# A two-layer attention and mixture-of-experts block: products that nobody reads, another order of stored queries and keys, and another pace of six experts

## The chip, the core and the metric

One core of a Trainium2 chip runs the whole program. The time is device microseconds of that core; a single run is one execution. Five engines work side by side: TensorE (PE: the matmuls; PEld: the loads of their stationary operands), VectorE (DVE), ScalarE (ACT), GpSimd (POOL) and SyncE (SP, which here only issues transfers). The profile gives the clock granted to TensorE as a share of full speed, PEclk.

## The reference, cut to what matters

Batch 2, 2048 tokens, width 256, in float32. Layer 0 is causal attention with 16 query heads of 16 numbers, 4 key heads and rotary embedding, beside 8 experts of which each token takes two. Layer 1 is attention over 32 learned patterns with sparsemax, beside 8 small experts and a shared one.

```python
xn = layernorm(x)
q = rope((xn @ Wqa @ Wqb).reshape(b, s, 16, 16))
k, v = split((xn @ Wkva @ Wkvb).reshape(b, s, 4, 16, 2)); k = rope(k)
w = softmax(where(causal, q @ repeat(k, 4).T / 4, -inf))
attn0 = (w @ repeat(v, 4)) @ Wout + bout
ffn0  = sum over the token's 2 experts e: gate * ((gelu(xn @ Wa[e]) * (xn @ Wg[e])) @ W_out[e])
x = x + attn0 + ffn0
xn = layernorm(x)
x = x + sparsemax_attention(xn, 32 patterns) + routed_and_shared_mlp(xn)
```

## The kernel before, in words

The span has three stages. The first, up to about 1434 us, makes layer 0's attention, routes the tokens, and runs the first six of layer 0's eight experts (`NIN = 6`) between the attention's matmuls. The second, from about 1461 us, runs experts 6 and 7. The third is layer 1.

**The list of the first stage.** Every instruction of the first stage is pinned in program order. A Python loop at the end of the stage (L1458) writes that order with a small model of the engines: `T` holds the time up to which each engine is taken, `on` and `pe` move it on, and `later`/`flush` hold jobs of the other engines until they are ready. At each step `candidates` (L1357) offers the next piece of each kind with a cost, and the cheapest is written. The kinds are: `score` (L564, the tile `sc`, one matmul, then exp on ACT into `es`), `values` (L579, tile `av`, 4 heads side by side), `maxima` (L515, tile `s`, two heads side by side with 64 rows each, then a maximum on DVE), the preparation of each 512 tokens (`normed` with tile `tp`, `lows` with `lw`, `tables` with `cs`, `rope_products` with `pab`, `make_v` with `pv`, `project` with `po`), and the experts' pieces (`ext`, `exh`, `exy`). A switch of kind costs 200 ns in the model. The constants at L1080 weigh the kinds.

**Products that nobody reads.** `product` (L1430) writes one bf16 matmul of 256 columns on a tile of ones into a PSUM tile (`idle`) that nobody reads. `fill` (L1440) writes them only ahead of the experts' first piece, and only where the model sees TensorE without work: after the preparation's first tile one for each `EACH` = 160 ns of such time, where the model's busy time of TensorE in the last `COUNT` = 3413 ns is under `SHARE` = 0.6 of it. In this count every piece is busy for its whole time, switches included.

**Queries and keys.** A rotary product is split into a high and a low part (fp32r); scores are the sum of the four products of parts, so a head takes 64 rows. `write_q` (L501) and `write_k` (L486) store each part twice in DRAM (`qd`, `kd`), SP issuing the transfers; `load_q` (L504) and `load_k` (L489) read them back into the tiles `q` and `ks` in two transfers each. `clean_q` and `clean_k` (L353, L356) fill unused rows first; `sel16` (L347) and `onecol` (L350), two small constants for this, are made on DVE.

**The end of the first stage.** The last `values` are followed by two transposes on DVE, `project`, and `add_sum` (L617), which adds attention's rows to `x1` in DRAM by a transfer of the POOL queue (`x<-xo`). Experts' results are added to the same `x1` by `ex_send` (L795, `x<-low,tox`); these transfers follow one another. The pace of the experts is the term `ahead` at L1391: the share of their pieces written less the share of the scores written since they began.

Of the kernel before, what the change touches and what calls it, by code (L numbers as in the profile page):

```python
# [149 lines left out]
def moe_transformer_kernel(  # L150
# [142 lines left out]
    with ExitStack() as actx:  # L293
# [34 lines left out]
        qsl = [attw.tile([P, 4, 512], F32R, name=f"q{i}") for i in range(NQS)]  # L328
        qd = [dram.tile([P, 4, 512], F32, name=f"qd{i}") for i in range(16)]
        kd = [dram.tile([64, 4, 512], F32, name=f"kd{i}") for i in range(8)]  # L330

# [14 lines left out]

        V.tensor_copy(sel16, bc(ident[0:16, 0:16], 1, [16, 8, 16]))  # L347
        for g in range(4):
            r0 = 64 - 64 * (g % 2) + 2 * (g // 2)
            V.tensor_tensor(onecol[:, g:g + 1], ident[:, r0:r0 + 1], ident[:, r0 + 1:r0 + 2], ALU.add)  # L350


        def clean_q(i):  # L353
            pin(G.memset(qsl[i].bitcast(F32), 0.0))

        def clean_k(i):  # L356

            for g in range(4):
                pin(A.activation(ksl[i][:, g].rearrange("p (a n) -> p a n", n=P), bc(ones, 1, [P, 4, P]), AF.Copy,
                                 scale=onecol[:, g:g + 1]))  # L360
# [9 lines left out]
        pin(A.dma_start(wa_sb[:, :, 96:96 + NE], wg.rearrange("(c p) m -> p c m", p=P)))  # L370
        pin(SP.dma_start(wkv16[64:96, 0:8], wkvb[:, 0:256].rearrange("k (v c) -> k v c", c=32)[..., 0:16]))
        pin(SP.dma_start(wq16, wqb.rearrange("k v t (g c) -> k v (t g) c", g=4)[..., 0:16]))
        pin(SP.dma_start(wkv16[64:96, 8:12], wkvb[:, 256:320].rearrange("k (g c) -> k g c", c=16)))
# [6 lines left out]
        for h in range(2):  # L380
            for r in range(2):
                hp = slice(64 * h, 64 * h + 64)
                pin(G.tensor_copy(identh[hp, r, 64 * r:64 * r + 64], ident[hp, hp]))
        pin(G.tensor_copy(trih, trif))
        number = attw.tile([P, 2, NTILE], I32, name="number")
# [100 lines left out]
        def write_k(b, blk, part, r):  # L486
            sdma(kd[4 * b + blk][:, r::2], bc(part.bitcast(F32), 1, [64, 2, 512]))

        def load_k(b, blk, ks):  # L489
            kss[b, blk] = ks  # L490
            for a in range(2):
                rows = kd[4 * b + blk].rearrange("(b a d) r n -> a (d r) b n", a=2, d=16)
                sdma(ks[64 * a:64 * a + 64, a::2].bitcast(F32), rows[a])

# [6 lines left out]
        def write_q(jp, part, r):  # L501
            sdma(qd[jp][:, 2 * r:2 * r + 2], bc(part.bitcast(F32), 1, [P, 2, 512]))

        def load_q(j, q):  # L504
            qs[j] = q
            for a in range(2):
                rows = qd[j // 2].rearrange("(t b a d) r n -> t a (d r) b n", t=2, a=2, d=16)
                sdma(q[64 * a:64 * a + 64, a::2].bitcast(F32), rows[j % 2, a])

# [5 lines left out]
        def maxima(j, i, kb):  # L515

            qb = j // 4 % 4
            if (i, kb) == (0, 0):
                parts[j] = atp.tile([P, 4, 4, 4], F32, tag="part", bufs=3, name="part")
            ks, q = kss[j // 16, kb], qs[j]  # L520
            n = 512 if kb < qb else P * (i + 1)
            tiles = []
            for pair in range(2):
                sc = ps2.tile([P, 2, 512], F32, tag="ps2", name="s1")
                tiles.append(sc)
                for h in range(2):
                    g = 2 * pair + h
                    mm(sc[:, h, :n], lhsT=q[half(g), g, P * i:P * i + P], rhs=ks[half(g), g, :n],
                       start=True, stop=kb < qb)
# [26 lines left out]
        def place_max(j):  # L556

            for a in range(2):
                r0 = 64 - 64 * a
                sdma(qs[j][r0:r0 + 4, a::2].bitcast(F32), bc(mrs[j][4 * a:4 * a + 4].bitcast(F32), 1, [4, 2, 512]))  # L560

        ess, avs, t3s, t3cs, rcs, atts, xos = {}, {}, {}, {}, {}, {}, {}

        def score(j, c, g):  # L564

            b, qb = j // 16, j // 4 % 4
            lo = max(0, c - 4 * qb) * P
            n = 512 - lo
            if g % 2 == 0:
                ess[j, c, g // 2] = esp.tile([P, 2, 512], F32, tag="es", name="es")  # L570
            es = ess[j, c, g // 2]
            sc = pssc.tile([P, 512], F32, tag="sc", name="sc")
            mm(sc[:, :n], lhsT=kss[b, c // 4][:, g, c % 4 * P:c % 4 * P + P], rhs=qs[j][:, g, lo:512], start=True, stop=True)
            pin(A.activation(es[:, g % 2, :n], sc[:, :n], AF.Exp, scale=0.25))  # L574
            if c >= 4 * qb and g % 2 == 1:
                pin(G.affine_select(es[:, :, 0:P], es[:, :, 0:P], pattern=[[0, 2], [1, P]], compare_op=ALU.is_ge,  # L576
                                    fill=0.0, base=0, channel_multiplier=-1))
# [227 lines left out]
        INF = 10 ** 9  # L805
        HOP, SWITCH, ISSUE, LAND, BYTE = 150, 200, 620, 2300, 0.003
        FULL = dict.fromkeys(("t", "l", "p", "f", "o"), "sc")
        T = dict.fromkeys(("PE", "V", "A", "G", "S", "D"), 0)
# [5 lines left out]
        def on(eng, dur, ready=0):  # L814
            T[eng] = max(T[eng], ready) + dur
            if eng == "PE":
                streamed.append((T[eng] - dur, T[eng]))
            return T[eng] + HOP

        def pe(mode, dur, ready=0):  # L820
            mode = FULL.get(mode, mode)
            dur += SWITCH * (mode != model["mode"])
            model["mode"] = mode
            return on("PE", dur, ready)

# [11 lines left out]
        def flush():  # L837
            now, done = T["PE"], False
            for job in sorted(jobs, key=lambda z: z[:2]):
                rank, _, eng, dur, ready, f, then = job  # L840
                if ready > now or (eng == "S" and T["S"] > now + ISSUE):
                    continue
                if eng == "AV":
                    eng = "A" if T["A"] <= T["V"] else "V"
# [70 lines left out]
        def start_fetch(grp):  # L915
# [3 lines left out]
            def landed(t):  # L919
# [5 lines left out]
                def go(k, t):  # L925
                    if k == len(steps):
                        at["x", grp] = t
                        later("S", ISSUE, t, lambda: keep_rows(grp), lambda t: x_done(grp, t), 2)
                    else:
                        if k < 6:  # L930
                            later("G" if k == 5 and grp > 1 else "V", costs[k], t, steps[k],
                                  lambda t: go(k + 1, t if 3 < k < 6 and grp > 1 else t - HOP), first)
                        else:
                            later("AV", (420, 350), t, steps[k], lambda t: go(k + 1, t - HOP), first)
                go(0, t)
# [72 lines left out]
        def k_load(b, kb, t):  # L1008
            later("S", 2 * ISSUE, t, lambda: load_k(b, kb, ksl[(4 * b + kb) % NKS]), lambda t: at.update({("k", b, kb): t}))

# [65 lines left out]
        for s, j in enumerate(order):  # L1076
            b, qb = j // 16, j // 4 % 4
            first_use.setdefault(("k", b, qb), s)
            first_use.setdefault(("q", j // 2), s)
        LEAD, MOST, EXB, SWX, RUN, ALONE, JOIN, IDLE, GAIN, GRP0, GRPN, QK0, QKN, FILL = 2.1, 20.0, 114.6, 109.1, 2, 130.6, 93.6, 61.9, 6119.2, 13.7, 2.9, 38.0, 3.1, -36.2  # L1080
        tab, made = set(), set()
# [275 lines left out]
        def candidates():  # L1357
# [30 lines left out]
            if ex["pos"] < len(pieces):  # L1388
                t = max(now, ex_ready())
                s0 = at.setdefault("ex0", model["scores"]) if t < INF else 0  # L1390
                ahead = ex["pos"] / len(pieces) - (model["scores"] - s0) / (all_scores - s0 + 1)  # L1391
                yield t - now + sw("sc") + EXB + GAIN * ahead, t, do_ex
# [21 lines left out]
        for i in range(3, NQS):  # L1414
            later("G", 2000, 3000 * i, lambda i=i: clean_q(i), None, 2)
        later("S", 9 * ISSUE, 40000, load_out_weights, None, 2)
# [19 lines left out]

        COUNT, SHARE, EACH = 3413, 0.6, 160
        gap = {"sum": 0, "n": 0}

        def fill(t1):  # L1440
# [4 lines left out]
            gap["sum"] += t1 - T["PE"]  # L1445
            while streamed and streamed[0][1] < t1 - COUNT:
                streamed.pop(0)
            have = sum(min(t1, e) - max(t1 - COUNT, s0) for s0, e in streamed)
            each = EACH if warm else 215 if T["PE"] < 7000 else 110
            while gap["sum"] > each:  # L1450
                gap["sum"] -= each
                if not warm or have < SHARE * COUNT:
                    have += 107
                    gap["n"] += 1
                    product()
                    streamed.append((t1 - 107, t1))

        while pos["av"] < len(avq) or jobs or projects or adds or scat["ti"] < NTILE or ex["pos"] < len(pieces) or not at.get("r0"):  # L1458
# [10 lines left out]
            if best and best[1] <= min(events + [INF]) + 400:  # L1469
                fill(max(T["PE"], best[1]))  # L1470
                best[2]()
            else:
                t1 = min(events) if events else T["PE"] + 500
# [1102 lines left out]
```

## Time and profile before

| | |
|---|---|
| median of 6 runs | 1995.09 us (1975.29 to 2010.63) |
| the profiled execution | 1999.27 us, of which the span is 1997.6 us |
| mean granted TensorE clock | 0.942 |
| DMA | 203.36 MB, mean 102 GB/s |
| of it `qd<-agx`, issues x size | 32 x 512 KB |
| `q<-qd` | 64 x 256 KB |
| `kd<-agx` | 16 x 256 KB |
| `ks<-kd` | 16 x 256 KB |
| exp, ACT `es<-sc` | x1280, mean 531 ns |
| maximum, DVE `part<-s` | x640, mean 1059 ns |

"Busy" of PE is the time in which at least one matmul is under way by modelled ends; a TensorE at half clock is busy too. The clock is shown for a stretch as a mean, 1.00 being full speed. Sizes of transfers are those of the data as written or read by the program.

### The profile page before, as it was taken

What the parts mean: (1) busy time and instruction counts of PE and PEld (TensorE: products, weight loads), DVE (VectorE), ACT (ScalarE), POOL (GpSimd) and SP (SyncE); (2) the same over time, 40 slices, a digit from 0 to 9 for tenths busy, and PEclk for the clock granted to TensorE, in tenths of its full rate; (3) what the DMA queues carried; (4) which work ended last, traced back from release to release, by engine and by line L of the source; (5) the groups of instructions that cost most, each with busy time, mean ns of one, the idle gap of its engine ahead of it and who ended that gap; (6) DMA issues with size and microseconds to landing.
All of it is one profiled execution on the core that took longest, in us unless ns stands there. A gap on an engine that the chain in (4) does not pass through costs nothing.

```text
span 1997.6 us, 28647 instructions
## 1 busy us (share of the span) xinstructions
PE 1902.1 (95%) x10472; PEld 1129.2 (57%) x10472; DVE 1242.9 (62%) x2546; ACT 1023.3 (51%) x1916; POOL 667.6 (33%) x849
## 2 busy tenths in 40 slices
PE   8989999999999999999999999999879899899996
PEld 5444443434556656566665556655556445578774
DVE  5576655577676665557756766663112559997275
ACT  4245323365656667666667666676511253344351
POOL 3223255562213223142222121212313108855651
PEclk8689666799999999999999999999989999999999
DMA  6537556651033233343322231211142402255547
GB/s 156 139 113 225 161 164 213 189 151 53 21 82 94 56 84 87 80 96 84 89 62 70 57 73 20 53 31 20 28 112 27 112 1 80 80 185 168 165 136 257
DMA packets 152969, 203.36 MB, mean 102 GB/s; under 512 B 15981, under 2 KB 120947, under 8 KB 152690
## 3 DMA queue, kind: packets, MB, share of 16 engines
q1 hardware_dynamic: 124498, 147.66, 25.1%
q0 software_dynamic: 27072, 53.08, 11.4%
q8 instruction: 87, 1.43, 0.3%
q10 hardware_dynamic: 1248, 0.67, 0.1%
q14 instruction: 64, 0.52, 0.1%
HBM read 102.44 MB, written 106.26 MB: 104 GB/s over the span
## 4 chain that ended last, share of the span: by engine, by line
PE 75%; DVE 9%; ACT 3%; issue 3%; DMA 2%; POOL 1%; SPq 0%; DVEq 0%; ACTq 0%; POOLq 0%
PE sc L336 16%; PE av L336 12%; PE s L336 10%; PE exh L336 9%; PE exy L336 4%; PE gu L142 4%; PE po L142 3%; DVE srt L142 3%; PE pab L336 3%; PE pz L142 2%; DVE part L535 2%; PE acc L142 2%; PE po L336 2%; PE pa L1582 1%; ACT es L574 1%
## 5 line engine op out<-in xcount | busy, mean ns | idle before, releaser
L574 ACT ACTIVATE es<-sc 128x512 f32<-128x512 f32 (+3 forms) x1280 | 634.0, 531 | 482.2 <-PE sc L336 457.8
L535 DVE TENSOR_REDUCE part<-s 128x2 f32<-128x1024 f32 (+3 forms) x640 | 650.4, 1059 | 274.7 <-PE s L336 273.1
L336 PE MATMUL sc<-q,ks 128*128 128x512 f32 (+3 forms) x1280 | 531.3, 469 | 12.0 <-ACT es L574 10.6
L336 PEld LDWEIGHTS sc<-q,ks 128*128 128x128 f32 x1280 | 222.8, 195 | 192.9 <-ACT es L574 93.7
L336 PE MATMUL av<-es,va 128*32 128x512 f32 (+3 forms) x2560 | 292.9, 554 | 4.3 <-POOL es L576 4.3
L576 POOL TENSOR_SCALAR_AFFINE_SELECT es<-es 128x256 f32<-128x256 f32 x256 | 109.1, 434 | 512.7 <-ACT es L574 509.9
L336 PE MATMUL s<-ks,q 64*128 64x512 f32 (+3 forms) x1280 | 235.3, 440 | 11.4 <-DVE part L535 3.7
L336 PEld LDWEIGHTS s<-ks,q 64*128 64x128 f32 x1280 | 106.8, 194 | 168.9 <-issue 71.2
L336 PEld LDWEIGHTS av<-es,va 128*32 128x32 f32 x2560 | 64.6, 110 | 121.7 <-issue 96.4
L796 POOL DMA_INDIRECT x<-low,tox x54 | 86.2, 1597 | 117.8 <-issue 51.1
L336 PE MATMUL exh<-cs_sb,low 128*128 128x256 f32 (+1 forms) x480 | 121.1, 359 | 0.0
L336 PE MATMUL exh<-cs_sb 128*128 128x256 f32 (+1 forms) x480 | 120.4, 360 | 0.0
L764 DVE COPY agx<-exh 128x512 f32<-128x512 f32 (+1 forms) x93 | 60.4, 649 | 96.1 <-PE exh L336 93.0
L142 POOL DMA_INDIRECT buf<-xn,slot x64 | 84.0, 1313 | 98.8 <-DVE cmp L142 79.6
L772 POOL TENSOR_TENSOR agx<-agx 128x1024 f32<-128x1024 f32 (+1 forms) x23 | 47.7, 2076 | 167.1 <-ACT agx L768 167.1
L142 POOL DMA_INDIRECT oe<-xn,to x72 | 78.6, 1091 | 46.9 <-ACT xn L142 29.5
L336 PEld LDWEIGHTS exh<-cs_sb,low 128*128 128x128 f32 x480 | 85.5, 189 | 13.2 <-ACT es L574 0.4
L336 PEld LDWEIGHTS exh<-cs_sb 128*128 128x128 f32 x480 | 84.9, 189 | 11.7
L142 DVE TENSOR_TENSOR srt<-srt 128x512 f32<-128x512 f32 (+6 forms) x104 | 75.9, 770 | 3.5 <-ACT srt L142 1.4
L721 POOL DMA_INDIRECT buf<-xsr,idx_sb x64 | 63.8, 997 | 27.1 <-DMA xsr<-xnd 9.2
L142 PE MATMUL gu<-xg,xn 128*128 128x256 f32 x288 | 66.4, 382 | 0.0
L142 DVE MAX8 srt<-z 128x8 f32<-128x16 f32 x768 | 60.5, 159 | 6.8 <-ACT z L142 6.8
(320 smaller groups left out, 2525.0 us busy)
## 6 DMA issues: line engine op xcount, KB each, us to landing
qd<-agx SPq DMA_DIRECT2D x32, 512.0 KB
q<-qd SPq DMA_DIRECT2D x64, 256.0 KB
buf<-zero SPq DMA_DIRECT2D x20, 516.0 KB
buf<-zero SPq DMA_DIRECT2D x20, 514.0 KB
xn<-buf SPq DMA_DIRECT2D x18, 514.0 KB
xsr<-xnd SPq DMA_DIRECT2D x32, 256.0 KB
oe<-zero SPq DMA_DIRECT2D x16, 512.0 KB
xn<-oe SPq DMA_DIRECT2D x16, 512.0 KB
```

What stands on the lines that cost most here:

```text
L142: return lambda *a, **k: self.tc.keep_in_program_order(f(*a, **k))
L336: pin(PE.matmul(*args, **kw))
L535: pin(V.tensor_reduce(parts[j][:, i, 2 * pair:2 * pair + 2, kb], sc[:, :, :n], AX.X, ALU.max))
L574: pin(A.activation(es[:, g % 2, :n], sc[:, :n], AF.Exp, scale=0.25))
L576: pin(G.affine_select(es[:, :, 0:P], es[:, :, 0:P], pattern=[[0, 2], [1, P]], compare_op=ALU.is_ge, fill=0.0, base=0, channel_multiplier=-1))
L721: pin(G.indirect_dma_start(ways[(2 * ti + k) % 8], bass.IndirectOffsetOnAxis(ap=idx_sb[:, k, ti:ti + 1], axis=0), xsr[:, ti % 3, k], None, ...
L764: pin((A.copy if eng == "A" else V.tensor_copy)(ag[i % 2][:, :, f, 0:n], exs["ps"][:, :, 0:n]))
L772: pin(eng.tensor_tensor(a, a, g, ALU.mult))
L796: pin(G.indirect_dma_start(x1[:], bass.IndirectOffsetOnAxis(ap=exs["to", i][:, c:c + 1], axis=0), ysx[:, c], None, compute_op=ALU.add))
L1582: PE.matmul(ps[:, :n], lhsT=wi[:, dc, col:col + P], rhs=inT[:, dc], start=dc == 0, stop=dc == 1)
```

## The change

Parts of the diff, in its order; names as above.

```diff
-        qd = [dram.tile([P, 4, 512], F32, name=f"qd{i}") for i in range(16)]
-        kd = [dram.tile([64, 4, 512], F32, name=f"kd{i}") for i in range(8)]
+        qd = [dram.tile([4, 2, 32, 512], F32, name=f"qd{i}") for i in range(16)]
+        kd = [dram.tile([2, 2, 32, 512], F32, name=f"kd{i}") for i in range(8)]
...
-        V.tensor_copy(sel16, bc(ident[0:16, 0:16], 1, [16, 8, 16]))
+        G.tensor_copy(sel16.rearrange("k v c -> k (v c)").rearrange("k (t d b) -> k t d b", d=16, b=2),
+                      ident[0:16, 0:16].unsqueeze(1).unsqueeze(3).broadcast_to([16, 4, 16, 2]))
...
-            V.tensor_tensor(onecol[:, g:g + 1], ident[:, r0:r0 + 1], ident[:, r0 + 1:r0 + 2], ALU.add)
+            G.tensor_tensor(onecol[:, g:g + 1], ident[:, r0:r0 + 1], ident[:, r0 + 1:r0 + 2], ALU.add)
+        def place(g):
+            return 2 * (g % 2) + g // 2
...
+        for dst, src in ((wkv16[64:96, 0:8], raw[1]), (wq16.rearrange("k v t c -> k (v t) c"), raw[0])):
+            pin(G.tensor_copy(dst.rearrange("k v c -> k (v c)").rearrange("k (t a d b) -> k t a d b", a=2, d=16, b=2),
+                              src.rearrange("k (t b a) d -> k t a d b", b=2, a=2)))
...
-            sdma(kd[4 * b + blk][:, r::2], bc(part.bitcast(F32), 1, [64, 2, 512]))
+            sdma(kd[4 * b + blk][:, r], part.bitcast(F32))
...
-                sdma(ks[64 * a:64 * a + 64, a::2].bitcast(F32), rows[a])
+                for r in range(2):
+                    r0 = 64 * a + 32 * r
+                    sdma(ks[r0:r0 + 32, 2 * a:2 * a + 2].bitcast(F32).rearrange("p b n -> p (b n)"), bc(rows[a, r], 0, [2, 16, 1024]))
...
-            sdma(qd[jp][:, 2 * r:2 * r + 2], bc(part.bitcast(F32), 1, [P, 2, 512]))
+            sdma(qd[jp][:, r], part.bitcast(F32))
...
+        STREAM = {"v": 0.45, "g": 0.2, "f": 0.8, "s": 0.85}
...
         def pe(mode, dur, ready=0):
+            part = STREAM.get(mode, 0.95)
             mode = FULL.get(mode, mode)
-            dur += SWITCH * (mode != model["mode"])
+            more = SWITCH * (mode != model["mode"])
             model["mode"] = mode
-            return on("PE", dur, ready)
+            t = on("PE", dur + more, ready)
+            streamed.append((T["PE"] - dur, T["PE"], part))
+            return t
...
-                        later("S", ISSUE, t, lambda: keep_rows(grp), lambda t: x_done(grp, t), 2)
+                        later("S", ISSUE, t + 1500, lambda: keep_rows(grp), lambda t: x_done(grp, t), 2)
...
-        LEAD, MOST, EXB, SWX, RUN, ALONE, JOIN, IDLE, GAIN, GRP0, GRPN, QK0, QKN, FILL = 2.1, 20.0, 114.6, 109.1, 2, 130.6, 93.6, 61.9, 6119.2, 13.7, 2.9, 38.0, 3.1, -36.2
+        LEAD, MOST, EXB, SWX, RUN, ALONE, JOIN, IDLE, GAIN, GRP0, GRPN, QK0, QKN, FILL, TAIL = 2.5, 20.0, 243.0, 215.8, 2, 62.2, 125.5, 72.4, 5092.0, 15.0, 5.5, 36.4, 2.7, 136.0, 11.8
...
-                ahead = ex["pos"] / len(pieces) - (model["scores"] - s0) / (all_scores - s0 + 1)
+                ahead = ex["pos"] / len(pieces) - (model["scores"] - s0) / (all_scores - s0 - TAIL)
...
-            later("G", 2000, 3000 * i, lambda i=i: clean_q(i), None, 2)
+            later("G", 2000, 30000, lambda i=i: clean_q(i), None, 2)
...
-        COUNT, SHARE, EACH = 3413, 0.6, 160
+        COUNT, SHARE, EACH, LEAST = 3413, 0.65, 150, 0.62
...
+        def share(t1):
+            while streamed and streamed[0][1] < t1 - COUNT:
+                streamed.pop(0)
+            return sum((min(t1, e) - max(t1 - COUNT, s0)) * w for s0, e, w in streamed)
...
+        def keep_up():
+            if ex["pos"] or ex["left"] or ("xt", 0) not in at:
+                return
+            while share(T["PE"]) < LEAST * COUNT:
+                gap["n"] += 1
+                product()
+                T["PE"] += 107
+                streamed.append((T["PE"] - 107, T["PE"], 1))
...
                 best[2]()
+                keep_up()
```

- `fill` counts with `share` too, at 0.65 and 150 ns. After every piece `keep_up` writes products until the counted share is 0.62, whether or not TensorE waits; a piece counts with its weight in `STREAM`, or 0.95, and a switch does not count. Both stop at the experts' first piece.
- Queries and keys are stored once, with a head's two neighbours interleaved; the loads read each row twice. The weights come into a part of `agx` and are put into the new order by two POOL copies; `sel16` and `onecol` are made on POOL. A load of `ks` is four transfers in place of two. `place` gives the new column of a head in `q` and `ks`, and `score`, `maxima`, `place_max` and `clean_k` use it.
- In the preparation, two kinds of DVE step (`VL`, `AVL` in `flush`) are written only where the model has POOL free, for up to 3 us.
- The experts' pace aims `TAIL` = 11.8 ahead of the end of the scores, in units of one chunk of 128 keys for 512 queries of 4 heads; every other weight of `candidates` but `MOST` and `RUN` is changed too, so the order of the first stage's pieces is another.

More of the change, by code (lines that the diff above doesn't have):

```diff
@@ L358, in clean_k @@
             for g in range(4):
-                pin(A.activation(ksl[i][:, g].rearrange("p (a n) -> p a n", n=P), bc(ones, 1, [P, 4, P]), AF.Copy,
+                pin(A.activation(ksl[i][:, place(g)].rearrange("p (a n) -> p a n", n=P), bc(ones, 1, [P, 4, P]), AF.Copy,
                                  scale=onecol[:, g:g + 1]))
@@ L370, in moe_transformer_kernel @@
         pin(A.dma_start(wa_sb[:, :, 96:96 + NE], wg.rearrange("(c p) m -> p c m", p=P)))
-        pin(SP.dma_start(wkv16[64:96, 0:8], wkvb[:, 0:256].rearrange("k (v c) -> k v c", c=32)[..., 0:16]))
-        pin(SP.dma_start(wq16, wqb.rearrange("k v t (g c) -> k v (t g) c", g=4)[..., 0:16]))
+        raw = [agx[rows, c0:c1].rearrange("p (v c) -> p v c", c=16) for rows, c0, c1 in ((slice(0, 64), 1024, 1536), (slice(64, 96), 1024, 1152))]
+        pin(SP.dma_start(raw[1], wkvb[:, 0:256].rearrange("k (v c) -> k v c", c=32)[..., 0:16]))
+        pin(SP.dma_start(raw[0].rearrange("p (v t) c -> p v t c", v=2), wqb.rearrange("k v t (g c) -> k v (t g) c", g=4)[..., 0:16]))
         pin(SP.dma_start(wkv16[64:96, 8:12], wkvb[:, 256:320].rearrange("k (g c) -> k g c", c=16)))
@@ L491, in load_k @@
             for a in range(2):
-                rows = kd[4 * b + blk].rearrange("(b a d) r n -> a (d r) b n", a=2, d=16)
-                sdma(ks[64 * a:64 * a + 64, a::2].bitcast(F32), rows[a])
+                rows = kd[4 * b + blk].rearrange("a r (d b) n -> a r d (b n)", b=2)
+                for r in range(2):
+                    r0 = 64 * a + 32 * r
+                    sdma(ks[r0:r0 + 32, 2 * a:2 * a + 2].bitcast(F32).rearrange("p b n -> p (b n)"), bc(rows[a, r], 0, [2, 16, 1024]))
         def q_products(jp):
@@ L506, in load_q @@
             for a in range(2):
-                rows = qd[j // 2].rearrange("(t b a d) r n -> t a (d r) b n", t=2, a=2, d=16)
-                sdma(q[64 * a:64 * a + 64, a::2].bitcast(F32), rows[j % 2, a])
+                rows = qd[j // 2].rearrange("(t a) r (d b) n -> t a (r d) (b n)", t=2, b=2)
+                sdma(q[64 * a:64 * a + 64, 2 * a:2 * a + 2].bitcast(F32).rearrange("p b n -> p (b n)"),
+                     bc(rows[j % 2, a], 0, [2, 32, 1024]))
         parts, mts, mrs = {}, {}, {}
@@ L527, in maxima @@
                     g = 2 * pair + h
-                    mm(sc[:, h, :n], lhsT=q[half(g), g, P * i:P * i + P], rhs=ks[half(g), g, :n],
+                    mm(sc[:, h, :n], lhsT=q[half(g), place(g), P * i:P * i + P], rhs=ks[half(g), place(g), :n],
                        start=True, stop=kb < qb)
@@ L559, in place_max @@
                 r0 = 64 - 64 * a
-                sdma(qs[j][r0:r0 + 4, a::2].bitcast(F32), bc(mrs[j][4 * a:4 * a + 4].bitcast(F32), 1, [4, 2, 512]))
+                sdma(qs[j][r0:r0 + 4, 2 * a:2 * a + 2].bitcast(F32), bc(mrs[j][4 * a:4 * a + 4].bitcast(F32), 1, [4, 2, 512]))
         ess, avs, t3s, t3cs, rcs, atts, xos = {}, {}, {}, {}, {}, {}, {}
@@ L572, in score @@
             sc = pssc.tile([P, 512], F32, tag="sc", name="sc")
-            mm(sc[:, :n], lhsT=kss[b, c // 4][:, g, c % 4 * P:c % 4 * P + P], rhs=qs[j][:, g, lo:512], start=True, stop=True)
+            mm(sc[:, :n], lhsT=kss[b, c // 4][:, place(g), c % 4 * P:c % 4 * P + P], rhs=qs[j][:, place(g), lo:512], start=True, stop=True)
             pin(A.activation(es[:, g % 2, :n], sc[:, :n], AF.Exp, scale=0.25))
@@ L815, in on @@
             T[eng] = max(T[eng], ready) + dur
-            if eng == "PE":
-                streamed.append((T[eng] - dur, T[eng]))
             return T[eng] + HOP
         def pe(mode, dur, ready=0):
+            part = STREAM.get(mode, 0.95)
             mode = FULL.get(mode, mode)
-            dur += SWITCH * (mode != model["mode"])
+            more = SWITCH * (mode != model["mode"])
             model["mode"] = mode
-            return on("PE", dur, ready)
+            t = on("PE", dur + more, ready)
+            streamed.append((T["PE"] - dur, T["PE"], part))
+            return t
         def shift(n, ready):
@@ L842, in flush @@
                     continue
-                if eng == "AV":
+                if eng in ("VL", "AVL"):
+                    held = T["G"]
+                    if eng == "VL":
+                        eng = "V"
+                        if held > now + 300 and now < ready + 3000:
+                            continue
+                    else:
+                        eng = "A" if T["A"] + 70 <= max(T["V"], held) else "V"
+                        if T[eng] > now + 300:
+                            continue
+                        dur, g = dur[eng == "V"], f
+                        f = lambda: g(eng)
+                    if eng == "V":
+                        ready = max(ready, held)
+                elif eng == "AV":
                     eng = "A" if T["A"] <= T["V"] else "V"
@@ L927, in go @@
                         at["x", grp] = t
-                        later("S", ISSUE, t, lambda: keep_rows(grp), lambda t: x_done(grp, t), 2)
+                        later("S", ISSUE, t + 1500, lambda: keep_rows(grp), lambda t: x_done(grp, t), 2)
                     else:
                         if k < 6:
-                            later("G" if k == 5 and grp > 1 else "V", costs[k], t, steps[k],
+                            later("G" if k == 5 and grp > 1 else "VL" if k == 4 else "V", costs[k], t, steps[k],
                                   lambda t: go(k + 1, t if 3 < k < 6 and grp > 1 else t - HOP), first)
                         else:
-                            later("AV", (420, 350), t, steps[k], lambda t: go(k + 1, t - HOP), first)
+                            later("AVL", (510, 350), t, steps[k], lambda t: go(k + 1, t - HOP), first)
                 go(0, t)
@@ L1008, in k_load @@
         def k_load(b, kb, t):
-            later("S", 2 * ISSUE, t, lambda: load_k(b, kb, ksl[(4 * b + kb) % NKS]), lambda t: at.update({("k", b, kb): t}))
+            later("S", 4 * ISSUE, t, lambda: load_k(b, kb, ksl[(4 * b + kb) % NKS]), lambda t: at.update({("k", b, kb): t}))
         def p_values(b, kb):
@@ L1445, in fill @@
             gap["sum"] += t1 - T["PE"]
-            while streamed and streamed[0][1] < t1 - COUNT:
-                streamed.pop(0)
-            have = sum(min(t1, e) - max(t1 - COUNT, s0) for s0, e in streamed)
+            have = share(t1)
             each = EACH if warm else 215 if T["PE"] < 7000 else 110
@@ L1455, in fill @@
                     product()
-                    streamed.append((t1 - 107, t1))
+                    streamed.append((t1 - 107, t1, 1))
+        def keep_up():
[6 more added lines that the diff above has]
+                streamed.append((T["PE"] - 107, T["PE"], 1))
         while pos["av"] < len(avq) or jobs or projects or adds or scat["ti"] < NTILE or ex["pos"] < len(pieces) or not at.get("r0"):
```

## The prediction

> **What bounds the kernel now.** I read the page's engine lines first, then busy time and clock by 50 us, then TensorE's timeline in one slow stretch, then the chain of waits at the end of the first stage.
>
> ```profile
> PE 1902.1 (95%) x10472; PEld 1129.2 (57%) x10472; DVE 1242.9 (62%) x2546; ACT 1023.3 (51%) x1916; POOL 667.6 (33%) x849
> ...
> PEclk8689666799999999999999999999989999999999
> ```
>
> TensorE is busy 95% of the span and bounds it. But 95% hides what a busy microsecond is worth: the clock row shows 0.6 to 0.8 in most of the first 8 slices (400 us), and full speed from there to the end of the first stage. Busy time and clock by stretch (columns: stretch, length, busy us and instructions of PE, PEld, DVE, ACT, POOL, then PEclk, DMA share, GB/s):
>
> ```profile
> 0.00:50.00 50.00, 42.27 (x215) 25.30 (x215) 27.67 (x79) 22.83 (x36) 19.05 (x40) 0.83 0.61 156
> 50.00:100.00 50.00, 47.38 (x228) 23.86 (x227) 29.19 (x51) 11.69 (x26) 11.19 (x15) 0.60 0.51 140
> 100.00:150.00 50.00, 44.63 (x287) 21.27 (x286) 37.91 (x78) 24.73 (x52) 12.53 (x48) 0.88 0.37 112
> 150.00:200.00 50.00, 45.66 (x306) 21.83 (x306) 33.53 (x76) 28.16 (x62) 17.23 (x54) 1.00 0.78 225
> 200.00:250.00 50.00, 48.41 (x208) 20.32 (x207) 32.67 (x55) 19.70 (x44) 14.83 (x21) 0.69 0.56 161
> 250.00:300.00 50.00, 48.05 (x163) 21.75 (x163) 27.72 (x39) 14.52 (x33) 29.44 (x34) 0.65 0.58 165
> 300.00:350.00 50.00, 47.75 (x186) 19.06 (x179) 28.40 (x31) 16.09 (x33) 26.98 (x33) 0.70 0.67 214
> 350.00:400.00 50.00, 48.52 (x223) 21.58 (x225) 28.38 (x30) 19.70 (x39) 29.07 (x38) 0.73 0.61 186
> 400.00:450.00 50.00, 47.15 (x290) 19.09 (x283) 36.09 (x44) 29.76 (x61) 31.62 (x49) 0.97 0.52 155
> ```
>
> In 200 to 400 us TensorE is busy 192.7 us of 200, yet puts out 163 to 223 instructions per 50 us against 306 at full clock in 150 to 200. No other engine is near full there. Lost clock in these nine rows, length times (1 - PEclk): 50 x 1.95 = 97.5 us. One slow stretch (297 to 319 us, mean clock 0.50; start, length, instruction):
>
> ```profile
> 299.54 1.08 PE L336 MATMUL av<-es,va 128*32 128x256 f32 x8
> 300.55 3.67 PE L336 MATMUL pab<-low,wkv 32*64 32x512 f32 x4
> 304.15 3.78 PE L336 MATMUL pab<-low,wq 64*128 64x512 f32 x4
> 307.86 1.96 PE L336 MATMUL pv<-wkv,low 32*128 32x64 f32 x8
> ```
>
> TensorE never pauses here, and still gets half the clock. What runs is narrow: rotary products use 32 or 64 of the 128 rows, `pv` 64 columns at a time. Rows of the unread products, which the list of before writes only into modelled idle time:
>
> ```profile
> L336 PE MATMUL idle<-ones x160: 269/285/437, 1.2 to 296.9; 128*128 128x256 bf16 x127, 64*128 64x256 bf16 x33
> ```
>
> Their last start is 296.9 us, and only two start after 200 us: the old count of streaming saw nothing missing where the clock was lost. The first stage's end, from the chain of waits:
>
> ```profile
> 1437.18 6.11 PE po L336 x14
> ...
> 1444.31 8.77 DMA x<-xo
> ...
> 1453.34 7.39 DMA x<-low,tox
> ...
> 1461.35 0.59 ACT inT L1571
> ```
>
> The attention's last sum and then an expert's last rows go out one behind the other, and the second stage starts only behind both.
>
> **The clock, the part that decides.** Work at full clock is busy times clock: 47.38 x 0.60 + 44.63 x 0.88 = 67.7 us in 50 to 150, and 133.4 us in 200 to 400 (33.4, 31.2, 33.4, 35.4). At the busy share of the full-clock row (45.66/50 = 0.913) these 201.1 us would take 220, not 300: at most 80 us to be had. That is a ceiling, since part of a matmul's length doesn't scale with the clock; no gain at all is the floor, if the added products don't lift it. How much do they lift? For: a switch no longer counts as streaming, `s`, `pv` and the logits' flips count for 0.85, 0.45 and 0.2, and products come without waiting for an idle gap, so any stretch rich in switches and small matmuls gets some. Against: a rotary product or a table counts 0.95 of its time, whatever its rows, and of the slow stretches those at 205 to 220, 250 to 280, 300 to 319 and 350 to 375 us have rotary products within or just ahead of them. Those keep losing the clock, though the stretch behind them should recover sooner. I take half the ceiling, since slow time splits about evenly between the two kinds: -40 us.
>
> The TensorE page of the Trainium skill, TensorE: Matmul & The Clock Gate, in its section on HAM oscillation, gives the rule as no idle gap over about 3.4 us. This trace has no such gap in 200 to 400 us (7.3 us are idle in all, in pieces) and a clock of 0.65 to 0.73 all the same, so it disagrees. By that rule the products could lift nothing, and the sum would be +3 us in place of -37.
>
> **What the products cost.** The row 9.04 to 15.90 us has 46 of them in 6.86 us, 149 ns each at a mixed clock; the list books 107. Their number isn't in the trace: none at the least; at the most 5 or 6 (0.17 of 3413 ns, if the count stands at 0.45, over 107) in each of the 132 lengths of 3.413 us in 450 us, some 700, which is 104 us at 149 ns. Nearer is one length in two asking for 2 (as TensorE is busy 85 to 97%): 130 products, 20 us. TensorE idles 15.3 us in the six slow rows (8.0 in 50 to 150, 7.3 in 200 to 400), and perhaps half of the products fall there: +10 us, from 0 to +30 in the likely case. If that cover is gone they cost 20.
>
> **The end of the stage.** `ahead` loses its `+ 1` and gains 11.8 units. At balance the experts stood EXB/GAIN = 114.6/6119 = 0.019 behind, now 243/5092 = 0.048, so most of the 11.8 is eaten, but the last `exy` (1443.11 us, 1.89 us, behind `po`) should come before the last `values`. Then the chain ends with `x<-xo`: 1461.35 - 1453.07 = 8.3 us off. What is late next is `x<-xo` itself; the rows of expert 6 (issued 1444.17, first used 1451.23) come earlier as well. Against it: chunks of scores without experts wait for ACT, four exps of about 0.61 us (2.44) against 4 x 0.23 + 0.99 = 1.91 us on TensorE, 0.53 us a chunk, at most 11.8 chunks or 6 us; I take 4 chunks, 2 us. Net -6 (from -8 to +2).
>
> **The start.** On DVE `sel` and `onecol` end at 7.07 us, behind POOL's memsets, and hold the first statistics (4.57, 2.50 us, against 0.39 for the next). On POOL they are five instructions of 0.2 to 0.3 us ahead of the memsets, about 1.2 us; the two reorder copies (nearest: 0.40 us for 256 elements, 1.26 for 512) add 2 us and wait for their weights behind the memsets that end at 6.74. POOL is idle for 11.83 us before 23.61, its next need, so that covers them; without it they would cost 3. -2.5 us for the statistics, at most. SP issues four transfers for a `ks` in place of two: 2 x 0.63 us ahead of the first `q` loads (37.97), whose landing the first `s` (43.82) awaits: +1.3 us; for all eight blocks 10 us of an SP that carries no link of the chain. Sum -1 (from -3 to +3). `keep_rows` 1.5 us later holds only `xsr<-xnd`, first issued at 263.3; the later `clean_q` (1.8 us) has POOL idle from 11.8 to 23.6 now, and in its new place stands before Newton steps (36.09) at worst: 0, or 1.8. The DVE steps now held until POOL is free do wait already (L214 took 2.42 us at 27.94, while POOL's L464 ran from 27.84 to 30.34); behind them on DVE stand maxima, which gain what the hold takes: 0, +-2.
>
> **Stored once, and the rest.** `qd` and `kd` shrink from 16.8 + 4.2 MB written to half, 10.5 MB less of 203. Where they run, DMA is 0.5 to 0.67 busy and no PE wait in 200 to 400 us is put down to a transfer: 0 (from -5, if loads there bring pieces forward, to +2, if rows read twice cost more). The new weights reorder the whole stage. Between 500 and 1400 us TensorE idles 9.3 us at full clock, so no order can win more there, and a worse one I bound by as much: 0, +-9.
>
> **The sum.** -40 + 10 - 6 - 1 = -37. On the profiled execution: 1999.3 - 37 = 1962 us. It lies 4.2 us above the median of the runs, so for the median 1995.1 - 37 = **1958 us**.
>
> **The rivals.**
> 1. *The clock is regained nearly everywhere.* For: 150 to 200 us has the same kinds, rotary products among them, at 1.00. Then -80, products +15, -7 for start and end: 1995 - 72 = 1923 us.
> 2. *The products go where the clock wasn't lost.* For: rotary products and tables still count 0.95, so what is narrow stays unfilled. Then perhaps 15 us of clock against 10 of products, with -7: 1983; with the end's gain gone too, 1989.
> 3. *Slower: products displace work.* `keep_up` moves `T["PE"]` on with no idle time behind it. If 300 products (over twice my count) stand in stretches already at full clock, 300 x 149 ns = 45 us, less 15 in idle time, less 7 at start and end: 1995 + 23 = 2018. It decides from the point at which the regained clock is worth less than the products in busy time plus those 7 us; the full-clock stretch 150 to 200, now 50 us for 306 instructions, shows it.
>
> **How the numbers follow.** Forecast 0.47, rival 1 0.16, rival 2 0.21, rival 3 0.16. The six runs spread from 1975 to 2011, so about 1% (20 us) is what a measurement tells from none. The forecast's own range is 1935 to 1980 (clock -25 to -60, products 0 to +20, the rest); nearly all of it and rival 1 are faster by over 1%: 0.63. Rival 2 and the forecast's weak edge are within 1%: 0.22. Rival 3, less its mild part: 0.15. The range from 1922 to 2008 leaves out half of rival 1 and most of rival 3.
>
> **What would show it.** PEclk in the first 8 slices: mean near 0.85 in 200 to 400 us for the forecast, over 0.95 for rival 1, under 0.75 for rival 2. Rows of `idle` after 50 us: some 100 to 200; over 300 with a longer full-clock stretch is rival 3. `exy` ends ahead of the last `av`, and `inT` follows `x<-xo`. `qd<-agx` shows 256 KB. The forecast is wrong if the clock stays where it is, or if experts begin later than now in spite of a better clock.

## The result, and the profile after

| | before | after |
|---|---|---|
| median | 1992.96 us (46 runs) | 2125.43 us (20 runs, 2120.38 to 2132.38) |
| ratio, 95% interval | | 1.0677 [1.0659, 1.0696] |
| span of the profiled execution | 1997.6 us | 2119.4 us |
| mean granted clock | 0.942 | 0.938 |
| products | 160 | 451 |

The change is 132 us slower where 37 us less was forecast, outside the range. From the page of after, the engine rows, the clock and DMA in 40 slices of 53 us, and the two groups of score matmuls (busy, mean ns; then TensorE's idle time just before them and what ended most of it):

```profile
PE 1920.2 (91%) x10763; PEld 1149.4 (54%) x10763; DVE 1244.6 (59%) x2551; ACT 1020.5 (48%) x1904; POOL 666.9 (31%) x858
...
PEclk8589877689899999999999999999999999999999
DMA  3134433444302231233333122221124311245547
...
L336 PE MATMUL sc<-q,ks 128*128 128x512 f32 (+3 forms) x1280 | 532.5, 468 | 74.2 <-ACT es L585 53.6
...
L336 PE MATMUL s<-ks,q 64*128 64x512 f32 (+3 forms) x1280 | 239.0, 440 | 37.2 <-DMA q<-qd 21.0
```

The same two groups before:

```profile
L336 PE MATMUL sc<-q,ks 128*128 128x512 f32 (+3 forms) x1280 | 531.3, 469 | 12.0 <-ACT es L574 10.6
...
L336 PE MATMUL s<-ks,q 64*128 64x512 f32 (+3 forms) x1280 | 235.3, 440 | 11.4 <-DVE part L535 3.7
```

TensorE's share fell from 95 to 91%: it now waits. Ahead of `sc` and `s` it stood idle for 12.0 and 11.4 us before, for 74.2 and 37.2 now, and 21.0 us of the 37.2 are put down to the loads of queries. Busy time and clock by stretch (columns as in the prediction):

```profile
50.00:100.00 50.00, 27.49 (x167) 18.52 (x164) 16.97 (x32) 2.74 (x5) 6.88 (x18) 0.50 0.16 61
100.00:150.00 50.00, 36.77 (x249) 20.22 (x249) 22.78 (x42) 15.15 (x34) 7.51 (x24) 0.83 0.37 116
...
300.00:350.00 50.00, 28.99 (x146) 13.48 (x146) 21.89 (x35) 9.77 (x23) 11.44 (x13) 0.79 0.28 99
350.00:400.00 50.00, 42.33 (x206) 20.16 (x206) 22.20 (x24) 16.30 (x35) 27.41 (x36) 0.73 0.54 161
400.00:450.00 50.00, 31.23 (x170) 13.68 (x172) 21.23 (x24) 13.29 (x29) 22.89 (x29) 0.83 0.32 99
```

In 50 to 100 us TensorE works for 27.5 us instead of 47.4, and at clock 0.50. DMA is busy 0.16 there. By these columns nothing is near full: the core waits for transfers while most of its DMA engines stand idle. The timeline of SP in after shows the other half of it (start, length, issues):

```profile
43.67 13.43 SPq L345 DMA_DIRECT2D q<-qd  x4
57.19 9.91 SPq L345 DMA_DIRECT2D kd<-agx  x2
67.19 7.50 SPq L345 DMA_DIRECT2D qd<-agx  x2
...
87.69 19.17 SPq L345 DMA_DIRECT2D wout_sb<-in_wout_dram  x8
```

and the same issues in before:

```profile
37.97 2.53 SPq L345 DMA_DIRECT2D q<-qd  x4
...
42.28 7.16 SPq L345 DMA_DIRECT2D wout_sb<-in_wout_dram  x8
```

Four issues that took 2.5 us take 13.4, and the eight of `wout_sb`, which the change doesn't touch, 19.2 in place of 7.2, as they stand behind the others. The DMA rows of the window 50 to 100 us tell why (40 slices of 1.25 us; tenths of 16 engines, then GB/s). After:

```profile
DMA  1111111111111111112222211111111111233211
GB/s 56 52 52 49 52 52 52 49 52 52 49 52 52 52 66 49 52 52 69 97 102 95 98 52 52 52 49 52 54 49 66 52 52 49 75 98 95 70 57 52
```

The queue is never empty and never fast: 52 GB/s in most slices, about 98 in a few. Two of 16 engines are 0.125, and 98 is nearly twice 52. The slowest index of a transfer is the outermost dimension of its access pattern that counts more than 1. In the storage of after it is 2 in the loads of `q` and `ks` (two copies of each row) and in the writes of `kd` (`a`), and 4 in the writes of `qd`. Such transfers are called narrow from here on, those with 16 or more wide. Reading: each such transfer runs on as many engines as that index counts. The Trainium skill has this rule, in DMA: Bandwidth & Descriptors, section "Why a DMA increments its semaphore by 16 and not by 1": the number of engines is the largest up to 16 that divides the slowest dimension other than 1 of both sides. The rows agree with it: 52 GB/s is 26 an engine, 98 is 24.5. The prediction did not draw on it.

### The profile page after: what moved, and what is told of

Same layout as the page of the kernel before. It is cut to its first block, busy times and chain, and to the rows that moved or that the text cites. A ratio compares the mean times of both kernels' runs of the same rounds, so it can differ in the third digit from the quotient of the medians.

```text
span 2119.4 us, 29249 instructions
## 1 busy us (share of the span) xinstructions
PE 1920.2 (91%) x10763; PEld 1149.4 (54%) x10763; DVE 1244.6 (59%) x2551; ACT 1020.5 (48%) x1904; POOL 666.9 (31%) x858
## 5 line engine op out<-in xcount | busy, mean ns | idle before, releaser
L336 PE MATMUL sc<-q,ks 128*128 128x512 f32 (+3 forms) x1280 | 532.5, 468 | 74.2 <-ACT es L585 53.6
L336 PE MATMUL s<-ks,q 64*128 64x512 f32 (+3 forms) x1280 | 239.0, 440 | 37.2 <-DMA q<-qd 21.0
L783 POOL TENSOR_TENSOR agx<-agx 128x1024 f32<-128x1024 f32 (+1 forms) x25 | 52.4, 2098 | 242.4 <-ACT agx L779 242.4
L336 PEld LDWEIGHTS exh<-cs_sb,low 128*128 128x128 f32 x480 | 85.3, 190 | 11.8
L336 PE MATMUL idle<-ones 128*128 128x256 bf16 (+2 forms) x451 | 86.4, 332 | 1.2 <-POOL ones L184 1.2
```

What stands on the lines that cost most here:

```text
L336: pin(PE.matmul(*args, **kw))
L783: pin(eng.tensor_tensor(a, a, g, ALU.mult))
```

## The experiments

The median of the kernel before lay between 1991 and 2038 us by chip, so each time is given as a ratio to it on the same chip, with a 95% interval. None of these kernels leaves work out. One point of ratio is 0.01, or 20 us.

**Storage: how many engines a transfer has.** *e1_wide* keeps everything of after, with its bytes, number of transfers and list, and orders the rows so that the slowest index of each write and load is 16 or more:

```diff
-        qd = [dram.tile([4, 2, 32, 512], F32, name=f"qd{i}") for i in range(16)]
-        kd = [dram.tile([2, 2, 32, 512], F32, name=f"kd{i}") for i in range(8)]
+        qd = [dram.tile([4, 16, 2, 2, 512], F32, name=f"qd{i}") for i in range(16)]
+        kd = [dram.tile([2, 16, 2, 2, 512], F32, name=f"kd{i}") for i in range(8)]
...
-            sdma(kd[4 * b + blk][:, r], part.bitcast(F32))
+            sdma(kd[4 * b + blk][:, :, r].rearrange("a d b n -> (a d) b n"), part.bitcast(F32))
...
-                      bc(rows[j % 2, a], 0, [2, 32, 1024]))
+                      bc(rows[j % 2, a], 1, [32, 2, 1024]))
```

> The change with its list of the first stage left as it is; only the order of qd and kd in DRAM and of the 64 rows of a head in q and ks is another, so that the slowest index of every write and load of queries and keys counts 16 or more, where the change has 2 (loads, and writes of keys) or 4 (writes of queries). Bytes and number of transfers are the change's. Theory A (narrow transfers are late): most of the 132 us goes, 1930 to 2000 us; PE idle in 50 to 150 us falls from 36 us to under 15, and SP's q loads take about 0.6 us each to issue again. Theory B (the added products and the new weights of the list cost the time): at least 2080 us. Theory C (the interleaved order itself, rows read twice): between, 2030 to 2080.

Measured 0.9882 [0.9802, 0.9961]: 8 points come back. The same DMA rows of the window 50 to 100 us, of e1_wide:

```profile
DMA  8639711240001991050000005995699900000014
GB/s 275 190 128 302 167 52 50 64 75 18 0 15 18 327 346 61 21 193 8 0 0 0 0 0 130 315 279 148 211 344 335 350 25 0 0 0 13 0 69 141
```

Bursts of 300 GB/s and pauses: the queue runs empty. Its stretches, to be set beside those of after:

```profile
50.00:100.00 50.00, 48.20 (x309) 30.04 (x306) 30.51 (x53) 11.00 (x25) 8.23 (x23) 0.69 0.38 117
...
300.00:350.00 50.00, 43.84 (x257) 20.45 (x257) 31.70 (x35) 19.68 (x44) 31.95 (x42) 0.93 0.48 150
```

Its issues on SP:

```profile
40.95 2.47 SPq L345 DMA_DIRECT2D q<-qd  x4
...
53.48 5.12 SPq L345 DMA_DIRECT2D wout_sb<-in_wout_dram  x8
```

TensorE works 48.2 us in place of 27.5, SP's four `q<-qd` issues are down from 13.43 to 2.47 us, and the unchanged `wout_sb` from 19.17 to 5.12. These are the signs of theory A, and in 50 to 150 us TensorE idles 5 us in place of 36. The row is still read twice, with the copy index moved inward: reading twice is not what costs.

*e2_q_narrow* is e1 with the copy index of the queries' loads outermost again (the diff's last pair the other way round, and the rows of `ks` in the matching order):

> As the run before, but the loads of queries alone have a slowest index of 2 again. Theory A, if the loads carry most of it (64 loads of 64 packets of 4 KB, 0.16 us each, on two engines in place of sixteen: 5.2 us a load): 2030 to 2100 us. If the writes of queries and keys and the loads of keys carry it: under 2000 us. Theory B: at least 2080 us, as the change.

Measured 1.011 [1.0013, 1.0207], two runs: the query loads alone cost 2.3 points (1.3 either way). That lies between the two announced ranges: loads and writes each carry a part. *e8_writes_wide* is after with its narrow loads and each write cut into transfers of 32 rows, 112 more issues on SP:

```diff
-            sdma(qd[jp][:, r], part.bitcast(F32))
+            for a in range(4):
+                sdma(qd[jp][a, r], part[32 * a:32 * a + 32].bitcast(F32))
```

> The change with its writes of queries and keys cut into transfers of 32 rows (four a part of queries, two of keys, slowest index 32), its loads left at two. Against the run with query loads alone narrow (e2, 1.011) it adds narrow key loads and 112 more issues on SP. If the narrow writes carry most of what is left (1.068 less 1.011): 1.01 to 1.03. If the key loads do: 1.05 or more.

Measured 1.0282 [1.0213, 1.0351]. By difference the narrow writes cost 1.0677 - 1.0282, 4.0 points or 79 us (0.7 points either way); the key loads 1.0282 - 1.011, 1.7 points or 34 us (1.2 either way), the additional issues among them; the query loads 2.3 points or 45 us. Only the 1.7 and the 2.3 are loosely known, as e2 and e8 have two runs each; the sum, 1.0677 - 0.9882, doesn't depend on them: 158 us of narrow transfers, behind an otherwise faster kernel.

*e3_store_only* is before with the change's storage alone, its weight copies and small constants included; *e4_old_store* is after with before's storage.

> The kernel before with the storage of queries and keys as in the change (with the two copies of the weights, and with sel16 and onecol on POOL), its weights, products and pace of experts left. Theory A: 2090 to 2150 us, as much slower as the change or more. Theory B: 1980 to 2005 us, no difference. The order of the pieces shifts a little, since the list counts the bytes of transfers; that alone should stay within 10 us.

> The change with the storage of the kernel before (every part written twice, loads over 64 rows), everything else of the change kept: products, new weights, pace of experts. Theory A: 1930 to 2000 us, near the forecast of 1958. Theory B: at least 2080 us.

Measured 1.0897 [1.0785, 1.1008] and 0.9852 [0.9776, 0.9928]. The change's storage costs 9.0 points in before's list and 8.3 in the change's (1.0677 - 0.9852), the same within the intervals. e1 and e4 have overlapping intervals: half the bytes written, on 16 engines, brought no gain that shows.

**The rest of the change.** The intervals of e4 and e1 hold the 37 us forecast for it. Stretches of e4_old_store:

```profile
250.00:300.00 50.00, 47.63 (x257) 23.38 (x256) 34.54 (x45) 19.45 (x42) 28.87 (x36) 0.86 0.73 218
300.00:350.00 50.00, 46.98 (x265) 20.98 (x265) 31.98 (x37) 20.60 (x45) 38.66 (x51) 0.93 0.65 213
350.00:400.00 50.00, 48.61 (x302) 21.84 (x302) 34.43 (x39) 28.18 (x57) 26.34 (x41) 1.00 0.56 157
```

0.86, 0.93 and 1.00, where before had 0.65, 0.70 and 0.73. *e5_wide_no_products* is e1 with before's rule for products; *e6_wide_old_weights* is e1 with before's weights of the list (`TAIL` kept); *e7_products_only* is before with the new rule alone; *e10_old_store_weights* is e4 with before's weights.

> The wide form (e1, 0.988 of the kernel before) with the rule and count for unread products of the kernel before: no products after every piece, 0.6 and 160 ns, switches counted. If the products regain the clock as the prediction has it (-40 +10): about 30 us slower than e1, ratio near 1.003, PEclk in 200 to 400 us back under 0.75. If the products are worth nothing: ratio 0.98 to 0.99, and the gain comes from the new weights. If they cost more than they bring: under 0.98.

> The wide form (e1) with the list's weights of the kernel before (LEAD to FILL), products, TAIL and the rest as in the change. The prediction gave the new weights nothing (0, +-9 us): ratio 0.984 to 0.993. If the new weights carry the gain: 1.00 or more. If they take some back: under 0.98.

> The kernel before with the change's rule and count for unread products alone. By the prediction's terms -40 + 10 = -30 us: ratio near 0.985, PEclk in 200 to 400 us above 0.80, some 450 products in all. If products need the new weights to help: 0.995 or more.

> Storage and list weights of the kernel before, all else of the change (products, TAIL, DVE steps held, sel16 and onecol as before). If storing once in the wide form is worth nothing: as e6, 0.980 to 0.990. If it brings something: 0.990 or more.

| kernel | ratio | products | clock lost in 0 to 450 us |
|---|---|---|---|
| before | 1 | 160 | 97.5 us |
| e1_wide | 0.9882 [0.9802, 0.9961] | 451 | 62 us |
| e5_wide_no_products | 1.001 [0.9975, 1.0045] | 173 | 86 us |
| e6_wide_old_weights | 0.9851 [0.9805, 0.9897] | 483 | 25 us |
| e7_products_only | 0.9973 [0.9944, 1.0002] | 486 | 52.5 us |
| e10_old_store_weights | 0.987 [0.982, 0.992] | 501 | 42.5 us |

Clock lost is the sum over the nine 50 us rows of length times (1 - PEclk), in the profiled execution. Without the products the wide form gains nothing (e5): they are worth 1.3 points, 26 us (0.9 points either way), in e1's list. The new weights are worth nothing that shows (e6 against e1, e10 against e4). e7 is the odd one, and missed its 0.985: 45 us of clock regained, 5 us of time, and its interval holds 1. That products need the new weights to help, the other reading announced for it, is not so: e6 and e10 have the old ones.

*e9_tail_only* is before with the term `TAIL` alone:

```diff
-                ahead = ex["pos"] / len(pieces) - (model["scores"] - s0) / (all_scores - s0 + 1)
+                ahead = ex["pos"] / len(pieces) - (model["scores"] - s0) / (all_scores - s0 - TAIL)
```

> The kernel before with TAIL = 11.8 in the pace of the experts, nothing else. The prediction's term is -6 us (8.3 off the chain, 2 back): ratio 0.997. In the profiles of the forms with TAIL the second stage's first matmul comes about 10 us after the last values matmul, against 29 in the kernel before: by these, -19 us, ratio near 0.990, less what the last scores lose without experts beside them (at most 6 us).

Measured 0.9972 [0.9938, 1.0006], -6 us, and the interval holds 1. Timeline of e9_tail_only at the end of the first stage (start, length, instruction; idle before it and releaser):

```profile
1453.53 0.69 DVE L615 TENSOR_TENSOR xo<-po,bout_sb 128x512 f32<-128x512 f32 x1 [2.43 <-PE po L336]
...
1454.28 1.09 PE L1569 MATMUL tp<-ident,low 128*128 128x128 f32 x8 [0.79 <-DVE xo L615]
...
1454.52 1.38 POOL L618 DMA_DIRECT2D x<-xo  x1 [7.88 <-DVE gates L1560]
1455.01 0.58 ACT L1571 COPY inT<-tp 128x512 f32<-128x512 f32 x1 [11.45 <-PE tp L1569]
```

The second stage's `tp` and `inT` start while `x<-xo` is only being issued. From the last `av` (1444.4) to the first matmul on `inT` (1456.2) it takes 11.8 us, against 29.6 in before (1434.1 to 1463.7). But the last `av` itself comes 10.3 us later. From 400 us to it TensorE idles 20.6 us in place of 16.3 and is busy 6.0 us longer; of these the expert's last `exy` (1.9 us), which stood behind the last `av` before, is one part, and the rest is not told apart.

**How many products.** *e11_rows_counted* is e6 with the matmuls on few rows counted for less; *e12_fewer_products* is e6 at lower shares, `SHARE` 0.55 and `LEAST` 0.52; *e15_rows_fewer* is e11 at 0.5 and 0.48.

```diff
-        STREAM = {"v": 0.45, "g": 0.2, "f": 0.8, "s": 0.85}
+        STREAM = {"v": 0.2, "g": 0.1, "f": 0.8, "s": 0.85, "c": 0.2, "r64": 0.3, "r128": 0.5}
```

> e6 (wide storage, old weights of the list) with rotary products, tables and values products counted by the rows they use (0.5 and 0.3 for 64 and 32 rows, 0.2 for 16 rows, pv 0.2, logits 0.1), so that the list writes 741 products in all in place of 483. If narrow matmuls lose the clock, PEclk in 0 to 450 us rises from a mean of 0.94 to above 0.97, worth at most 25 us of e6's lost clock; 258 more products at 0.15 us cost up to 39 us where nothing is idle. Ratio 0.98 to 1.00; under 0.98 if the clock pays.

> e6 with the shares lowered to 0.52 (after every piece) and 0.55 (in idle time), so 285 products in place of 483. If products in busy time are a cost that is not all needed: the clock holds and the ratio falls to 0.975 to 0.983. If each is needed: the clock falls and the ratio rises to 0.99.

> e11 (narrow matmuls counted by their rows) with the shares at 0.48 and 0.50: 346 products in place of 741. If what e11 lost (0.993 against e6's 0.985, at a clock of 0.989) was the cost of its 258 more products: 0.975 to 0.985 here. If not: 0.985 to 0.993.

| kernel | products | mean clock, lowest to highest run | ratio |
|---|---|---|---|
| e12_fewer_products | 285 | 0.961 to 0.972 | 0.987 [0.9826, 0.9914] |
| e15_rows_fewer | 346 | 0.978 to 0.980 | **0.9813 [0.9779, 0.9846]** |
| e6_wide_old_weights | 483 | 0.968 to 0.977 | 0.9851 [0.9805, 0.9897] |
| e11_rows_counted | 741 | 0.985 to 0.989 | 0.9929 [0.9906, 0.9953] |

e12's ratio lies between its two announced ranges, and its interval reaches both: leaving out 198 of e6's products lost nothing that shows. e11 buys nearly the whole clock and pays more than it is worth. Two of its stretches:

```profile
250.00:300.00 50.00, 49.93 (x303) 28.10 (x302) 25.89 (x30) 16.52 (x36) 39.68 (x45) 1.00 0.68 217
300.00:350.00 50.00, 46.96 (x326) 22.46 (x330) 36.69 (x43) 23.89 (x50) 30.02 (x46) 1.00 0.57 160
```

e15, which counts as e11 does and writes fewer products in all, has a higher clock in every run than e6 with its 483: where the products stand counts, and not only how many there are. It has the lowest ratio here, 1961.38 us against 1997.94 of before on its chip; its interval lies wholly below 1 and overlaps those of e6, e12 and others.

**Products and `TAIL` together.** *e13_products_tail* is e7 with `TAIL`; *e14_products_tail_hold* adds the held DVE steps.

> The kernel before with the rule for products and TAIL, nothing else. If the two add up (0.9973 and 0.9972 alone): 0.9945. If together they bring what e10 shows (0.987), the rest of the change being nothing: 0.984 to 0.990.

> As e13, and the two kinds of DVE step of the preparation held until POOL is free. The prediction gave the hold nothing (0, +-2 us): the same as e13 within 0.003. If the hold carries what is missing between the sum of parts (0.9945) and e10 (0.987): 0.987 here and 0.9945 in e13.

Measured 0.9882 [0.9848, 0.9915] and 0.9844 [0.98, 0.9888]. e13 is better by 0.6 points than e7 and e9 added up (0.9973 + 0.9972 - 1 = 0.9945), just more than the three intervals together allow (0.56 points). So the two parts seem to help one another. The traces show where: in e7 the first matmul on `inT` follows the last `av` by 28.3 us (1434.5 to 1462.8), in e13 by 8.9 (1433.0 to 1441.9), and in e13 the last `av` does not come later for it, as it did in e9. TensorE idles 9 us less in e13 than in e7 before 600 us, and its experts begin at 428.1 us in place of 443.4. Why `TAIL` does that to the list these runs do not show. The hold's 0.4 points lie within the overlap of the intervals.

## Why the prediction was wrong

**The step that failed** is "Stored once, and the rest": "DMA is 0.5 to 0.67 busy and no PE wait in 200 to 400 us is put down to a transfer: 0 (from -5 …, to +2 …)". It counted bytes. It did not look at the shape of a transfer, which was in the diff: `bc(rows[j % 2, a], 0, [2, 32, 1024])`. At 52 GB/s a 256 KB load lasts 5 us, and the first four `q` loads stand one behind the other. The term, put at 0, measured +158 us (after against e1). A quiet transfer queue told of the old shapes and bounded nothing for the new ones. The sentence on SP, "10 us of an SP that carries no link of the chain", fell with it: SP was made to wait by its own queue, and what stood behind it came late. No rival held this case, so the range could not reach it. The announced sign "if experts begin later than now in spite of a better clock" came half: the first `ext` starts at 575.8 us in place of 473.7, and the clock is no better (116 us lost in the first 600 us, 97.5 before). There TensorE idles 130 us, 34 before; e1, the same list with wide transfers, idles 32 and loses 62 us of clock, so the waits cost clock too. Of the other signs, `exy` does end ahead of the last `av` (1555.9 and 1574.6 us), `qd<-agx` shows 256 KB, and 333 rows of `idle` start after 50 us, more than the forecast's 100 to 200.

**The clock, -40**: right in size. With wide transfers 48 (e4) or 62 us (e1) are lost in place of 97.5, and e7 alone regains 45; in 200 to 400 us PEclk means 0.91 in e4 (0.86, 0.86, 0.93, 1.00), against "near 0.85" for the forecast. The rule on idle gaps, by which products could lift nothing, does not hold here: e7, e6, e10 and e11 raise the clock with them.

**The products, +10**: their number was too low, and their price depends on the list. The list wrote 291 to 341 more, not 130. e7 regains 45 us of clock and ends 5 us sooner, so by estimate its 326 cost some 40 us, 0.12 each, if a us of clock regained is a us of time. TensorE's idle time up to the last `av` went from 43.6 us in before to 48.4 in e7, so nothing shows that half of them fell into idle time. This is the mechanism of rival 3 (300 products, 45 us), without its sign. In e1's list it is otherwise: against e5 it has 278 products more, regains 24 us of clock and gains 26 us of time, and TensorE's idle time up to the last `av` falls from 60.0 to 47.8; there the products cost nothing that shows. e12 shows that 198 of the 323 that e6 adds to before's bought nothing that shows.

**The end, -6**: the sum agrees (e9, -6 us, with an interval from -12 to +1), both parts were off, and that they cancel is luck. The chain shortened by 29.6 - 11.8 = 17.8 us, not 8.3, as the second stage starts without waiting for `x<-xo`, so the announced sign that `inT` follows `x<-xo` did not come. Against it stand 10.3 us by which the last `av` comes later, not 2, of which 4.3 are idle time of TensorE, the only part that the prediction had.

**The new weights, 0, and the hold, 0**: no run contradicts them (e6 and e1; e14 and e13). **The start, -1**: no run isolates it. **Rival 1 and 2** were about the clock alone; the runs lie between them. So the sum without its failed term, -37, is -24 in e1 and -29 in e4 with intervals that hold it, in part by luck, as over twice the products were written and the two parts of the end cancelled; and 158 us of narrow transfers stand on top.

## What to carry to other kernels

Halving the bytes of a transfer is worth nothing if its pattern's slowest index shrinks to 2 or 4, below the 16 DMA engines: read that index off both sides of every changed transfer before counting bytes, and put a broadcast's copy index inside it. A low DMA share beside waits for DMA, and an SP whose issues grow long, are the sign of it. Products that keep the clock up can cost busy time: look which of them buy clock, since here 346 made a faster kernel than 741.

## What the runs showed of the hardware

A few narrow transfers delay the wide ones behind them on the same queue: `wout_sb`, unchanged in shape, took 2.4 us an issue (19.17 / 8) in place of 0.9 (7.16 / 8), and 0.6 in e1 (5.12 / 8), where all are wide. A TensorE that is hardly idle can have half its clock: in before it was busy 21.5 of the 22 us from 297 to 319, at 0.50, on rotary products of 32 and 64 rows and other small matmuls. That the few rows are the cause is not shown by itself; what speaks for it is that products placed by such rows bought more clock, 0.978 to 0.980 with 346 (e15) against 0.968 to 0.977 with 483 (e6).
